# Attention with an octonion FFN on one Trainium2 core: score stacks filled in strided rows, and the q and k weights loaded behind the store of the parts

## The chip, the cores and the metric

The kernel runs as one program on one core of a Trainium2 chip. The metric is the device time of one execution in microseconds (us). "PE" is TensorE's matmul, "PEld" its weight load, "DVE" VectorE, "ACT" ScalarE, "POOL" GpSimd and "SP" SyncE, which in this kernel does little but issue DMA transfers.

## The reference, cut to what matters

Two sequences of 1024 tokens with 512 features go through a layer norm; the result feeds causal attention of 32 heads of 16 features with an ALiBi bias, and a feed-forward network whose weights are ternary and multiplied as octonions. The output is `x + s * g`.

```python
xn = _layernorm(x)                                    # x: 2 x 1024 x 512
# attention, 32 heads of 16
qkv = jnp.einsum('bsd,od->bso', xn, w_qkv) + b_qkv
scores = jnp.einsum('bqhd,bkhd->bhqk', q, k) * (1 / sqrt(16))
scores = scores + slopes[h] * positions[k]            # ALiBi
scores = jnp.where(causal, scores, -1e9)
out = softmax(scores) @ v
s = jnp.einsum('bsd,od->bso', out, w_out) + b_out
# feed-forward network
h = silu(oct_ternary_linear(xn, w_gate)) * oct_ternary_linear(xn, w_up)
g = silu(oct_ternary_linear(h, w_down))
x = x + s * g
```

## The kernel before

**Work and units.** The attention is cut into units (b, g, qc): sequence b, group g of four heads (eight groups), half qc of the 1024 queries. There are 32 units. For each unit PE computes scores twice. The first pass (line 553, tiles `s1`, in the profile `s<-k_stack,q_stack`) serves only the row maxima, which DVE takes (`mx`, `left`). The maxima are turned by PE (line 618, `pm`), copied by ACT (`mr`) and written by a DMA that POOL issues into rows 126 and 127 of the query stack. The second pass (line 669, tiles `s2`, with a mask product at line 688 for blocks on the diagonal) then has scores less their maximum, and ACT takes the exponentials `p`. Line 707 multiplies `p` by `v`, and line 776 is the output projection. After the attention come the products of the network (lines 1436 and 1478).

**Stacks.** A score is a product over a stack of rows. `q_stack` (a ring of 4) and `k_stack` (a ring of 5) hold 128 partitions x 4 heads x 512 tokens. Rows 0 to 63 are four parts of 16 rows each: high and low parts of q or k, so that high x high, high x low, low x high and low x low are added up in one product. Rows 64 and 65 hold the ALiBi bias in two parts, and rows 126 and 127 the maxima. The order of the 64 rows is free as long as both stacks have the same.

**Where the rows come from.** `qk_items` (line 461) computes q and k of a set, which is two groups of one sequence. There are eight sets, n = 0 to 7. A set has four blocks (q and k, each in two halves of 512 tokens), and a block has four matmuls (line 477, tile `pqk`). After a block ACT adds the bias and rounds to the high part, DVE computes the low part (both go to `st`), and SP stores the block to DRAM (`sp<-st`, 512 KB). `fill_k` (line 514) and `fill_q` (line 527) read from there: four transfers of 128 KB on SP for one stack half, each 16 partitions x 4 heads x 512 tokens in pieces of 2 KB, and for `k_stack` one more for the bias rows.

**Weights of a set.** `load_wq` (line 143) issues two transfers of 512 KB on SP into `wqr`. `compact_wq` (line 151) has POOL copy them in eight pieces into `wq`, which the matmuls read; it is called ahead of the first product of the set. Both tiles have a single buffer. The load for set n + 1 is issued in `product`, at the last product of set n.

**What sets the order.** Every engine runs its instructions in the order of the program. That order is decided while the program is built by a planner written out in Python: at each step it looks at the candidates (a maximum's product, an exponential's product, a value product, a transpose, a side item such as a product of `qk_items`) with an estimate of when each is ready, and emits one. Its clock is `now`, in ns. For a fill it keeps `link`, the estimate of when the fill has gone out on the DMA link, and `fill_at`, when the stack can be read; `next_max` places a product of the first pass no earlier than `fill_at` of its stack. The planner has no estimate for the weights in `wqr`. Fills are issued by `try_fill` (line 1136).

Of the kernel before, what the change touches and what calls it, by code (L numbers as in the profile page):

```python
# [10 lines left out]
F32 = mybir.dt.float32  # L11
# [8 lines left out]
B, S, D = 2, 1024, 512  # L20
NT = B * S
H, HD = 32, 16
NG = H // 4
KD = D // P
# [51 lines left out]
def kernel(  # L76
# [21 lines left out]
    act_, dve_, pool_, sp_ = (  # L98
        InOrder(tc, engine, held) for engine in (nc.scalar, nc.vector, nc.gpsimd, nc.sync)
    )  # L100
# [3 lines left out]
    def pe(ins):  # L104

        return tc.keep_in_program_order(ins)

    NP = NG // 2
# [34 lines left out]
    def load_wq(gp, eng):  # L143
        t = wqp.tile([P, 2, KD, 2, 4, 32], F32, tag="wqr", name=f"wqr_{gp[0]}_{gp[1]}")
        for n in range(2):
            eng.dma_start(
                out=t[:, n].rearrange("p k w h e -> p (k w h e)"), in_=wqk[2 * gp[1] + n]
            )
        wq_raw[gp] = t

    def compact_wq(gp):
        t = wq_raw.pop(gp)
        w = wqp.tile([P, KD, 2, P], F32, tag="wq", name=f"wq_{gp[0]}_{gp[1]}")
        for n in range(2):
            for k in range(KD):
                pool_.tensor_copy(
                    w[:, k, :, n * 64 : (n + 1) * 64].rearrange("p w (h d) -> p w h d", d=HD),
                    t[:, n, k, :, :, 0:HD],
                )
        wq_tiles[gp] = w  # L160
# [59 lines left out]
    for n in range(2):  # L220
        pool_.dma_start(
            out=bqk_sb[n * 64 : n * 64 + 64, 1 - n : 1 - n + 2 * NG],
# [183 lines left out]

    def q_of(b, g, half):
        return q_ring[(2 * (b * NG + g) + half) % 4]  # L410

    def k_of(b, g, half):
        return k_ring[(2 * (b * NG + g) + half) % 5]
# [47 lines left out]
    def qk_items(b, gp):  # L461

        box = {}

        def product(which, c, kt):
            if (which, c, kt) == (0, 0, 0):
                if (b, gp) not in wq_tiles:
                    compact_wq((b, gp))
                parts[b, gp] = [
                    spill.tile([2, P, S], F32, tag=f"sp{w}", name=f"sp_{b}_{gp}_{w}")  # L470
                    for w in range(2)
                ]
            if kt == 0:
                box["ps"] = ps_m.tile([P, 512], F32, tag="m", name=f"pqk_{b}_{gp}_{which}_{c}")
            ps = box["ps"]
            pe(
                nc.tensor.matmul(  # L477
                    ps,
                    lhsT=wq_tiles[b, gp][:, kt, which, :],
                    rhs=xnT[:, kt, b * S + c * 512 : b * S + (c + 1) * 512],  # L480
                    start=(kt == 0),
                    stop=(kt == KD - 1),
                )
            )
            n = b * NP + gp + 1
            if (which, c, kt) == (1, 1, KD - 1) and n < B * NP:
                load_wq((n // NP, n % NP), sp_)
            if kt < KD - 1:
                return
            bias = bqk_sb[:, 1 + 2 * (which * NP + gp) :][:, 0:1]  # L490
            st = stg.tile([P, 2, 512], F32R, tag="st", name=f"st_{b}_{gp}_{which}_{c}")
            act_.activation(st[:, 0, :], ps, AF.Identity, bias=bias)
            dve_.scalar_tensor_tensor(
                st[:, 1, :], ps, bias, st[:, 0, :].bitcast(F32), ALU.add, ALU.subtract
            )
            sp_.dma_start(
                out=parts[b, gp][which][:, :, c * 512 : (c + 1) * 512].rearrange(
                    "l p n -> p l n"
                ),
                in_=st.bitcast(F32),  # L500
            )

        return [
            (858, lambda w=w, c=c, kt=kt: product(w, c, kt), "qk" if kt == KD - 1 else None)
            for w in range(2)
            for c in range(2)
            for kt in range(KD)
        ]

    def heads(t, l, g, first, n):  # L510
        lo = (g % 2) * 64
        return t[l, lo : lo + 64, first : first + n].rearrange("(h d) n -> d h n", d=HD)

    def fill_k(b, g, half):

        k = k_of(b, g, half)
        for r in range(4):
            sp_.dma_start(
                out=k[r * HD : (r + 1) * HD].bitcast(F32),
                in_=heads(parts[b, g // 2][1], r % 2, g, half * 512, 512),  # L520
            )
        sp_.dma_start(
            out=k[64:66].bitcast(F32),
            in_=al_dram[:, 4 * g : 4 * g + 4, half * 512 : half * 512 + 512],
        )

    def fill_q(b, g, half):

        q = q_of(b, g, half)
        for r in range(4):  # L530
            sp_.dma_start(
                out=q[r * HD : (r + 1) * HD].bitcast(F32),
                in_=heads(parts[b, g // 2][0], r // 2, g, half * 512, 512),
            )

# [2 lines left out]
    def max_items(b, g, qc):  # L538
# [7 lines left out]
        def products(tl, first, count, c, n):  # L546
            x_banks[0] += 1
            ps = ps_x.tile(
                [P, 512], F32, tag=f"x{x_banks[0] % 3}", name=f"s1_{b}_{g}_{4 * qc + tl}_{c}_{first}"
            )  # L550
            for j in range(count):
                pe(
                    nc.tensor.matmul(  # L553
                        ps[:, j * n : (j + 1) * n],
                        lhsT=q_of(b, g, qc)[0 : NR - 2, first + j, tl * P : (tl + 1) * P],
                        rhs=k_of(b, g, c)[0 : NR - 2, first + j, :n],
                        start=True,
                        stop=True,
                    )
                )  # L560
            return ps[:, 0 : count * n].rearrange("p (h n) -> p h n", n=n)
# [50 lines left out]
    def place_max(b, g, qc, tiles):  # L612

        q = q_of(b, g, qc)
        ps = ps_m.tile([P, 512], F32, tag="m", name=f"pm_{b}_{g}_{qc}")
        for tl in range(4):
            pe(
                nc.tensor.transpose(  # L618
                    ps[0:8, tl * P : (tl + 1) * P],
                    tiles["rm"][:, tl].rearrange("p l h -> p (l h)"),  # L620
                    ident,
                )
            )
        mr = wk.tile([8, 512], F32R, tag="mr", name=f"mr_{b}_{g}_{qc}", bufs=1)
        act_.copy(mr, ps[0:8, :])
        for n in range(2):
            pool_.dma_start(
                out=q[NR - 2 + n : NR - 1 + n].bitcast(F32),
                in_=mr[4 * n : 4 * n + 4, :].bitcast(F32),
            )  # L630
# [218 lines left out]
    def unit_of(lst, n):  # L849
        return lst[n][0] if n < len(lst) else NU  # L850

    for b in range(B):
        for hh in range(2):
            n = 2 * b + hh
# [11 lines left out]
        for gp in range(2 - 2 * b, NP):  # L866
            n = b * NP + gp
            u = 4 * n
            add(
                qk_items(b, gp),  # L870
                u - 6 if n > 1 else -1,
                u - 3,
                lambda b=b, n=n: n < 2 or fills[0] >= 4 * (2 * n - 2) and (b == 0 or not waits_x()),
            )
# [23 lines left out]
    for n in order:  # L898
        if n in seen:
            continue  # L900
        k = n
# [90 lines left out]

    busy(20)
    qk, vs = qk_items(0, 0), v_items(0, 0)

    def issue(items):
# [62 lines left out]
    lead_in += [(d // 4, None, it) for d, it in zip(due, vs)]  # L1059
    head_v = len(lead_in)  # L1060
    lead_in += [(size[0] + 4 * d, None, it) for d, it in zip(due[::2], qk_items(0, 1))]
    known["l", "g"] = 36000
    known["k", "u"] = 42000
# [43 lines left out]
    now, kind = [HEAD], ["F"]  # L1107
# [3 lines left out]
    p_ready, placed, fill_at = {}, {}, []  # L1111
    link = [0.0]
# [20 lines left out]
    qk_done = [HEAD + 4500]  # L1133

    def try_fill():

        n, part = divmod(fills[0], 4)
        if n >= B * NG or len(qk_done) <= (n // 2 + 1 if n > 1 else part // 2):
            return
        if n == 0 and now[0] < qk_done[part // 2] - 4000:  # L1140
            return
        if unit_of(exps, E[0]) < 2 * (n - 2) + (0, 1, 2, 2)[part]:
            return
        (fill_q if part % 2 else fill_k)(n // NG, n % NG, part // 2)
        fills[0] += 1
        link[0] = max(now[0], link[0], qk_done[n // 2 + 1 if n > 1 else part // 2]) + (4500 if n else 3000)
        fill_at.append(link[0] + 2500)

    def try_fetch():
        for n, k in enumerate(fetches):  # L1150
# [213 lines left out]
    while E[0] < len(exps) or V[0] < len(vals) or S_[0] < len(side) or norms or behind:  # L1364
        try_fill()
        try_fetch()
        if not w_again and unit_of(exps, E[0]) >= NU - 5:
            fetch_signs()
        if not step():
            now[0] += 500  # L1370
            assert now[0] < 1e8
# [245 lines left out]
```

## Time and profile before

| | |
|---|---|
| median of 3 runs | 1092.06 us (1090.71 to 1093.07) |
| profiled execution | 1090.84 us, its span 1089.0 us |
| mean granted TensorE clock | 0.98 of full speed |
| DVE, ACT, POOL busy | 678.9, 508.3, 173.8 us |
| DMA | 104.04 MB, mean 96 GB/s over the span |
| fills | 128 transfers of 128 KB each into `k_stack` and into `q_stack` |
| weights | 16 transfers of 512 KB into `wqr` |

The span runs from the first to the last instruction; the rest of the profiled execution's time lies around it. Times inside the profile count from the start of the span. A wait is idle time of an engine just before an instruction, put down to what released that instruction. The granted clock is the share of full speed that TensorE got in a stretch. The DMA share is the mean busy share of the core's 16 DMA engines, GB/s what they moved.

The attention's first units run from about 37 us on; the products of the network's output end the span. All 32 stores of `st` lie between 19 and 650 us.

### The profile page before, as it was taken

Reading aid. Unit: us, or ns where it says so; the run is one execution under the profiler, and the core shown is the slowest. Engines: PE = TensorE matmul, PEld = TensorE weight load, DVE = VectorE, ACT = ScalarE, POOL = GpSimd, SP = SyncE. Lnnn points to the kernel's source line nnn. Section 1 sums busy time; section 2 is a strip of 40 time slices with the busy share of each in tenths; the row PEclk is TensorE's granted clock in tenths of the full one; section 3 lists DMA queues with packets and bytes.
Section 4 is the critical chain, followed back from the end, with each engine's and each line's share of the span. In section 5 each row is a group of like instructions: output and inputs, shape, how many; then the busy total and the mean of one; then the engine's idle time right before and its main releaser. Section 6 shows DMA issues by size and latency. Waiting matters only on the chain.

```text
span 1089.0 us, 15459 instructions
## 1 busy us (share of the span) xinstructions
PE 1036.4 (95%) x5578; PEld 696.3 (64%) x5578; DVE 678.9 (62%) x1406; ACT 508.3 (47%) x958; POOL 173.8 (16%) x288
## 2 busy tenths in 40 slices
PE   8798988998999999999999999999999999999995
PEld 5554656674666667556667566665456678888784
DVE  6668888774988867878878778858342123141312
ACT  4032647654665544555645455665581213232322
POOL 7501014001010011010011000010011123332322
PEclk9999979999999999999999999999999999999998
DMA  6986563525374454355354337741141113030211
GB/s 226 175 157 161 137 124 108 89 52 116 82 154 89 123 85 81 99 136 95 74 128 65 82 78 116 137 89 50 35 132 49 49 59 116 1 116 1 79 38 39
DMA packets 73195, 104.04 MB, mean 96 GB/s; under 512 B 25896, under 2 KB 30640, under 8 KB 73120
## 3 DMA queue, kind: packets, MB, share of 16 engines
q1 hardware_dynamic: 69648, 98.28, 40.2%
q0 software_dynamic: 3424, 4.64, 1.7%
q8 instruction: 45, 0.74, 0.3%
q14 instruction: 30, 0.25, 0.1%
q10 hardware_dynamic: 48, 0.13, 0.0%
HBM read 69.39 MB, written 33.10 MB: 94 GB/s over the span
## 4 chain that ended last, share of the span: by engine, by line
PE 76%; DVE 8%; issue 5%; DMA 5%; ACT 4%; POOL 2%; SPq 0%; DVEq 0%; POOLq 0%; ACTq 0%
PE po L707 12%; PE s L669 12%; PE s L553 11%; PE pqk L477 9%; PE pu L1436 6%; PE pg L1436 6%; PE pd L1478 6%; PE pout L776 5%; PE pv L435 4%; DVE mx L69 3%; PE s L688 2%; DMA q_stack<-mr 1%; ACT p L69 1%; PE pm L618 1%; DVE s L69 1%
## 5 line engine op out<-in xcount | busy, mean ns | idle before, releaser
L69 ACT ACTIVATE p<-s 128x512 f32<-128x512 f32 x576 | 317.5, 596 | 205.0 <-PE s L688 114.0
L669 PE MATMUL s<-q_stack,k_stack 128*128 128x512 f32 (+3 forms) x768 | 252.5, 397 | 10.3 <-ACT p L69 5.1
L553 PE MATMUL s<-k_stack,q_stack 126*128 126x512 f32 (+3 forms) x768 | 235.5, 391 | 15.3 <-DVE mx L69 7.7
L69 DVE TENSOR_REDUCE mx<-s 128x1 f32<-128x384 f32 (+3 forms) x352 | 226.2, 643 | 11.6
L69 DVE TENSOR_REDUCE left<-s 128x1 f32<-128x512 f32 x256 | 163.8, 684 | 49.7 <-PE s L553 49.3
L669 PEld LDWEIGHTS s<-q_stack,k_stack 128*128 128x128 f32 x768 | 133.1, 190 | 82.7 <-ACT p L69 37.3
L553 PEld LDWEIGHTS s<-k_stack,q_stack 126*128 126x128 f32 x768 | 131.3, 192 | 67.5 <-issue 23.0
L707 PE MATMUL po<-p,v 128*32 128x512 f32 (+3 forms) x1536 | 142.2, 492 | 0.4 <-ACT p L69 0.4
L69 DVE TENSOR_TENSOR s<-s,mask 128x128 f32<-128x128 f32 (+2 forms) x352 | 123.9, 352 | 29.0 <-PE s L553 28.1
L477 PE MATMUL pqk<-xnT,wq 128*128 128x512 f32 x256 | 132.3, 618 | 8.1 <-POOL wq L69 6.9
L69 DVE SCALAR_TENSOR_TENSOR h<-pu,sc_u,sg 128x512 f32<-128x512 f32 (+1 forms) x44 | 33.0, 751 | 156.6 <-PE pu L1436 155.6
L69 POOL DMA_DIRECT2D q_stack<-mr x64 | 32.2, 508 | 615.5 <-ACT mr L69 615.5
L69 POOL TENSOR_TENSOR hs<-h,hs 128x512 fp32r<-128x512 f32 (+1 forms) x43 | 56.3, 1310 | 215.5 <-ACT hs L69 215.5
L688 PE MATMUL s<-mask_r,ident_r 128*128 128x256 f32 (+1 forms) x320 | 89.0, 278 | 0.0
L707 PEld LDWEIGHTS po<-p,v 128*32 128x32 f32 x1536 | 42.3, 109 | 72.5 <-issue 65.3
L69 ACT ACTIVATE sg<-pg,sc_g 128x512 f32<-128x512 f32 (+1 forms) x44 | 30.2, 687 | 100.2 <-PE pg L1436 100.0
L435 PE MATMUL pv<-wv,xnT 128*128 128x256 f32 x256 | 68.3, 392 | 0.1
L477 PEld LDWEIGHTS pqk<-xnT,wq 128*128 128x128 f32 x256 | 46.4, 195 | 33.8 <-issue 20.3
L69 ACT CAST hs<-h 128x512 fp32r<-128x512 f32 (+1 forms) x44 | 27.2, 619 | 85.3 <-DVE h L69 85.3
L776 PE MATMUL pout<-wo_sb,oT 128*128 128x512 f32 x128 | 62.7, 604 | 0.5 <-ACT oT L69 0.5
L688 PEld LDWEIGHTS s<-mask_r,ident_r 128*128 128x128 f32 x320 | 60.5, 189 | 2.7 <-issue 1.7
L435 PEld LDWEIGHTS pv<-wv,xnT 128*128 128x128 f32 x256 | 47.0, 193 | 17.1 <-issue 8.4
(144 smaller groups left out, 1074.8 us busy)
## 6 DMA issues: line engine op xcount, KB each, us to landing
sp<-st SPq DMA_DIRECT2D x32, 512.0 KB
k_stack<-sp SPq DMA_DIRECT2D x128, 128.0 KB
q_stack<-sp SPq DMA_DIRECT2D x128, 128.0 KB
wqr<-in_wqk_dram SPq DMA_DIRECT2D x16, 512.0 KB
xt<-in_x_dram SPq DMA_DIRECT2D x16, 256.0 KB
att<-o SPq DMA_DIRECT2D x32, 128.0 KB
ot<-att SPq DMA_DIRECT2D x16, 256.0 KB
proj<-y SPq DMA_DIRECT2D x16, 256.0 KB
```

Of the source, the lines that this page charges most:

```text
L69: ins = issue(*args, **kwargs)
L435: nc.tensor.matmul(ps[:, 0:256], lhsT=xnT[:, c, b * S + kt * P : b * S + (kt + 1) * P], rhs=wv_tiles[2 * b + hh][:, c, :], start=(c == 0), ...
L477: nc.tensor.matmul(ps, lhsT=wq_tiles[b, gp][:, kt, which, :], rhs=xnT[:, kt, b * S + c * 512 : b * S + (c + 1) * 512], start=(kt == 0), st ...
L553: nc.tensor.matmul(ps[:, j * n : (j + 1) * n], lhsT=q_of(b, g, qc)[0 : NR - 2, first + j, tl * P : (tl + 1) * P], rhs=k_of(b, g, c)[0 : NR ...
L618: nc.tensor.transpose(ps[0:8, tl * P : (tl + 1) * P], tiles["rm"][:, tl].rearrange("p l h -> p (l h)"), ident,)
L669: nc.tensor.matmul(ps[:, c0 : c0 + w], lhsT=k_of(b, g, kt // 4)[0:NR, h, kt % 4 * P : (kt % 4 + 1) * P], rhs=q[0:NR, h, 512 - w : 512], st ...
L688: pe(nc.tensor.matmul(out, lhsT=ident_r, rhs=rhs, start=False, stop=True))
L707: nc.tensor.matmul(po[32 * i : 32 * i + 32, 512 - w : 512], lhsT=v[:, kt, h * VC : h * VC + 32], rhs=p[:, i * part + c0 : i * part + c0 + ...
L776: nc.tensor.matmul(ps, lhsT=turned[t][:, c, :], rhs=wo_sb[0][:, c, :], start=(c == 0), stop=(c == KD - 1),)
L1436: nc.tensor.matmul(ps[:fs, :], lhsT=fw[mt][:, n0 + kt, 0:fs], rhs=part[:, kt, :], start=(kt == 0 and n == 0), stop=(kt == KD - 1 and n == 1),)
L1478: nc.tensor.matmul(pd, lhsT=hs[k][:fs, n, st * P : (st + 1) * P], rhs=fw[mt][:fs, 8:12, :].rearrange("p s n -> p (s n)"), start=(mt == 0 a ...
```

## The change

Three things change. The four transfers of a fill no longer write 16 consecutive rows each: transfer r writes rows r, r + 4, r + 8 and so on up to r + 60, in both stacks alike. The load of the next set's weights is issued after the store of the last block instead of before its bias, low part and store. And the planner's estimates for a fill get shorter: `link` moves by 2600 ns a fill instead of 4500 (3000 for the first group), and the stack counts as readable 2200 ns after that instead of 2500.

```diff
@@ qk_items, product
-            n = b * NP + gp + 1
-            if (which, c, kt) == (1, 1, KD - 1) and n < B * NP:
-                load_wq((n // NP, n % NP), sp_)
             if kt < KD - 1:
                 return
             bias = bqk_sb[:, 1 + 2 * (which * NP + gp) :][:, 0:1]
...
                 in_=st.bitcast(F32),
             )
+            n = b * NP + gp + 1
+            if (which, c, kt) == (1, 1, KD - 1) and n < B * NP:
+                load_wq((n // NP, n % NP), sp_)
@@ fill_k
         for r in range(4):
             sp_.dma_start(
-                out=k[r * HD : (r + 1) * HD].bitcast(F32),
+                out=k[r:64:4].bitcast(F32),
                 in_=heads(parts[b, g // 2][1], r % 2, g, half * 512, 512),
             )
@@ fill_q
         for r in range(4):
             sp_.dma_start(
-                out=q[r * HD : (r + 1) * HD].bitcast(F32),
+                out=q[r:64:4].bitcast(F32),
                 in_=heads(parts[b, g // 2][0], r // 2, g, half * 512, 512),
             )
@@ try_fill
         fills[0] += 1
-        link[0] = max(now[0], link[0], qk_done[n // 2 + 1 if n > 1 else part // 2]) + (4500 if n else 3000)
-        fill_at.append(link[0] + 2500)
+        link[0] = max(now[0], link[0], qk_done[n // 2 + 1 if n > 1 else part // 2]) + 2600
+        fill_at.append(link[0] + 2200)
```

Since the planner works with these estimates, the order of the other instructions on every engine moves as well; their number on PE stays the same.

## The prediction

> **What bounds the kernel now.** I read the page's busy times first, then PE's waits over two stretches, then the windows around the fills and around the waits, then the chain and SyncE's timeline.
>
> Busy times (engine, us, share of the span, instructions):
>
> ```profile
> PE 1036.4 (95%) x5578; PEld 696.3 (64%) x5578; DVE 678.9 (62%) x1406; ACT 508.3 (47%) x958; POOL 173.8 (16%) x288
> ```
>
> PE is the bound; only 1089.0 - 1036.4 = 52.6 us of its span are idle, so an edit on another engine pays only where PE stands still or runs at half clock. PE's waits from 0 to 260 us (who, on what: us in total, times, longest), then from 260 to 715:
>
> ```profile
> PE pqk L477 <- POOL wq L69: 5.8, 2, 3.2
> PE s L553 <- DMA q_stack<-sp: 5.6, 2, 5.2
> PE s L669 <- DMA q_stack<-mr: 4.2, 2, 2.4
> ```
>
> ```profile
> PE pqk L477 <- POOL wq L69: 1.1, 1, 1.1
> ```
>
> A fill (`q_stack<-sp`) makes PE wait only near the start, and between 260 and 715 us it never does: there the fills are hidden, and whatever new wait the change puts there is lost whole. The windows of the fill stage (window, its length, busy time and count of PE, PEld, DVE, ACT, POOL; then granted clock, DMA share, GB/s):
>
> ```profile
> 31.00:36.00 5.00, 5.00 (x24) 4.24 (x23) 1.60 (x3) 0.69 (x1) 4.95 (x3) 1.00 1.06 135
> 36.50:40.50 4.00, 4.00 (x24) 3.48 (x23) 2.67 (x5) 0.00 (x0) 3.51 (x39) 1.00 1.04 416
> 45.00:53.00 8.00, 2.84 (x11) 1.69 (x11) 6.61 (x14) 0.00 (x0) 0.00 (x0) 0.95 1.07 131
> ```
>
> All DMA engines are busy in all three, but while fills run (31 to 36, 45 to 53) only 131 to 135 GB/s move, and 416 while other loads run. A fill of 512 KB takes 512 KiB / 131 GB/s = 4.0 us. Behind PE's waits the clock falls:
>
> ```profile
> 53.05:59.00 5.95, 5.95 (x13) 3.80 (x13) 3.18 (x8) 0.00 (x0) 0.00 (x0) 0.50 1.06 130
> 93.20:96.60 3.40, 3.40 (x5) 1.51 (x5) 1.48 (x3) 0.00 (x0) 0.66 (x3) 0.50 0.95 251
> 249.44:254.00 4.56, 4.56 (x8) 2.02 (x9) 0.00 (x0) 0.00 (x0) 0.66 (x3) 0.63 0.44 61
> 477.43:482.00 4.57, 4.57 (x26) 2.79 (x26) 2.85 (x5) 2.66 (x5) 0.66 (x3) 1.00 1.02 253
> ```
>
> These follow PE waits of 5.20, 2.62, 3.18 and 1.08 us: the first leaves 6 us at half clock (3.0 us lost), the next two 3.4 us each (1.7 lost), the last nothing. The chain (start, length) shows what the early waits stand on, and SyncE's timeline how stores and weight loads are queued:
>
> ```profile
> 33.79 8.37 DMA sp<-st
> ...
> 62.50 7.97 DMA q_stack<-mr
> ...
> 87.18 5.62 DMA wqr<-in_wqk_dram
> ```
>
> ```profile
> 86.26 0.36 SPq L69 DMA_DIRECT2D sp<-st  x1
> 86.71 1.29 SPq L69 DMA_DIRECT2D wqr<-in_wqk_dram  x2
> 92.61 0.38 SPq L69 DMA_DIRECT2D sp<-st  x1
> ```
>
> The store of set 0's last block, issued at 33.79, landed at 42.16 because two slow fills and 1 MB of `wqr` were ahead of it, and the next fills start only then. At 62.5 a `mr` transfer of 8 KB took 7.97 us behind six fills (median landing 2.3 in the list of issues). And `wqr` is on the path already: issued at 86.71, landed at 92.80, first of it copied into `wq` by POOL, PE running again at 93.20. The next store went out only at 92.61, after it; the change turns these two round.
>
> **Part 1, strided rows.** Same instructions and bytes; only the partitions of each of the four transfers differ. No row shows this pattern. One end: nothing changes (131 GB/s). Other end: as fast as the other loads, 416 GB/s. I take a doubling, 262 GB/s and 2.0 us a fill: the 16 consecutive rows now lie four times as far apart, and issuing a fill takes SyncE 1.75 us (42.18 to 43.91 for four), so beyond a doubling the issue itself would bound.
>
> [...]
>
> What it gives at the start: together with part 2 the store of 33.79 no longer stands behind 1 MB of weights (2.5 us at 416 GB/s) and two fills are 4 us shorter; it lands near 37, and unit 1's first fills by about 45 instead of 52.8. PE's wait of 5.20 and the half clock after it go, and so does most of the 7.97 us of `mr`. What is late next is DVE: its timeline runs without a gap from 38.1 to 51.8 us on unit 0's maxima, and only then are `rm`, PE's transpose (0.6), ACT's `mr` (0.6), POOL's issue (0.9) and a landing of 2.3 to 4 us possible. That puts the first product of the exponentials (L669) at 57 to 60, I take 58.6, instead of 70.6: 12.0 us earlier, less 1.3 us of PE work that the new order leaves for later: **-10.7**. Bounds: -8.0 (landing and order 2.7 worse) to -13.3 (57.3, and nothing left over).
>
> **Part 2, the load behind the store.** In the built order each of the seven later `wqr` loads stands behind the last store of its set on SyncE, and that store waits for ACT and DVE. Rows for the path from the last product of a set to PE's next restart: ACT 0.69, DVE 0.75, issue 0.1 (together 1.54; 2.68 to 2.87 in the first two sets); store to next issue 0.46 (92.61 to 93.08); load, issue to landing 6.1 (86.71 to 92.80; other sets 5.3 to 6.2 by their last packet); copies until PE runs 0.4. So 8.5 us, early 9.8. All of it is hidden where the order puts that much PE work between two sets; queued behind the held products on PE are the scores of the next units, so ACT and DVE starve too. At four of the seven boundaries there is enough (the wait of 3.18 us ahead of set 3 is not one on the load: POOL stands there behind a `mr` transfer in both orders, and it stays). At three there isn't:
> - Set 1 to 2: one score product in between (0.2 us). Wait 8.3 to 9.6, I take 8.8, instead of 2.62: **+6.2**. Half clock follows in both; 0 to 1.7 more.
> - Set 3 to 4: the new order leaves 12 value products (1.7 us by the row of 2.29 for 16), 4 transposes (0.5), 5 products of L669 and 2 masks (1.3), 3 of L553 (0.7), 4.2 us in all; wait 8.5 - 4.2, I take 4.1 (3.5 to 5.6) and 1.7 of half clock: **+5.8**. Before, no wait.
> - Set 5 to 6: 4 products of L669, 2 masks and 3 short ones of L553, 1.5 us; wait 7.0 instead of 1.08, and 1.7 of half clock (3.4 if it falls as behind 5.20): **+7.6** (6.8 to 9.3).
>
> [...]
>
> **Part 3, the planner's constants.** They cost no instruction; they let a score product be placed 4.8 us (2600 + 2200 ns) behind a fill's issue, where it was 7.0 (4500 + 2500). With fills 2.0 us shorter this is safe in the sum. PE has the same 4461 instructions in the built order, three fewer changes into value products; -0.6 at most. From 137 to 205 us, where PE stands in small waits that end on DVE or `mr` (one of 1.78), the faster `mr` and fills give **-1.5** (0 to -3). The rest, with another tail of the attention after 720 us: **-1.0** (-2.8 to +2; new fill waits up to +3).
>
> **Sum.** -10.7 + 6.2 + 5.8 + 7.6 - 1.5 - 1.0 = +6.4 us. On the profiled execution (1090.84 us: span 1089.0 and 1.84 around it) that is 1097.2. The median of the runs, 1092.06, lies 1.2 above the profiled one, so on its basis **1098.4 us**. All terms at their best: -13.3 + 5.7 + 5.2 + 6.8 - 3.0 - 2.8 = -1.4, or 1090.7; at their worst -8.0 + 8.7 + 7.3 + 9.3 + 5 = +22, which needs all to go wrong at once.
>
> **Rivals.**
> 1. *Faster: the start gives much more.* Elapsed time less PE's work stands at 24.7 us at 88 us, 6.7 of it from before the first score product. If all the other 18.0 went, and 5.0 of the small waits from 137 to 205 us, the sum is -18.0 - 5.0 - 1.0 + 19.6 = -4.4, or 1087.7. It decides from a start gain of 17 us on. For it: DMA is saturated from 43 to 66 us. Against: DVE's unbroken row to 51.8 us.
> 2. *The same: gain and stalls cancel*, within 2.2 us of 1092.06 (0.2%, about what a measurement of this kernel can tell from no change). With every load at 5.3 us the three stalls cost 17.7 by the ends above, and with the best start it is -13.3 + 17.7 - 1.5 - 1.0 = +1.9, or 1094.0; for it: the load of set 6 in the trace of before took 5.3. Against: both ends at once.
> 3. *The fills don't get faster.* Then the start gives only the 2.5 us of weights ahead of the store, and the constants are too early by up to 2.2 us a unit where a fill is late: -2.5 + 19.6 + 0 to 5, or 1109 to 1114. For it: all DMA engines are busy already during fills, with nothing in the trace that says why they are slow. Against: other loads reach 416 with the same engines.
> 4. *The load behind the store isn't felt*, because the next products are placed far enough away: the order shows it for four boundaries, not for three; included in rivals 1 and 2.
>
> **How the numbers follow.** My sum 0.64, rival 1 0.20, rival 2 0.10, rival 3 0.06. The forecast's own range is 1094.5 to 1104, from the ends of the start gain and of the three stalls, not all at once. The range for 8 in 10 takes in rival 2 and most of rival 1: 1087.5 to 1105.5. Slower is the forecast and rival 3: 0.70; same 0.10; faster 0.20.
>
> **What would show it.** Right: some 260 GB/s in the windows of fills; no `s <- DMA q_stack<-sp` near 50 us; first L669 near 58.6; `pqk <- POOL wq` grown from 6.9 us in three waits to some 23 us in four, each new one at a set boundary and followed by half clock. Wrong: a start gain over 17 us, 131 GB/s as before, or waits on `wq` under 10 us in total.

## The result and the profile after

The changed kernel takes 1099.42 us (median of 4 runs, 1098.8 to 1099.56) against 1091.99 us for the kernel before (4 runs, 1090.71 to 1093.07): 1.0067 times as long, 95% interval 1.005 to 1.0085. The forecast was 1098.4 us and slower. The profiled execution took 1099.45 us, its span 1097.7.

Busy times of the changed kernel (engine, us, share of the span, instructions):

```profile
PE 1035.5 (94%) x5578; PEld 695.7 (63%) x5578; DVE 678.7 (62%) x1406; ACT 508.6 (46%) x958; POOL 173.5 (16%) x288
```

PE runs the same 5578 instructions in a span that is 8.7 us longer. Its busy time is 0.9 us less and its idle time grows from 52.6 to 62.2 us, so the loss is time in which PE stands still. Its waits from 0 to 260 us and, in the second fence, from 260 to 715 (who, on what: us, times, longest). The line numbers are higher by one:

```profile
PE pqk L478 <- POOL wq L69: 13.2, 2, 9.9
PE s L554 <- DVE mx L69: 4.6, 5, 2.5
PE s L554 <- DVE rm L69: 1.9, 1, 1.9
```

```profile
PE pqk L478 <- POOL wq L69: 14.3, 3, 7.6
```

The waits on `q_stack<-sp` and `q_stack<-mr` are no longer in the list; those on `wq` have grown from 6.9 us in three to 27.4 (13.2 + 14.3 with rounding) in five. They stand at the set boundaries that were named, as PE's timeline shows (start, length, instruction, in brackets the idle time before it and who ended it; from set 1 to 2, 3 to 4, 5 to 6):

```profile
91.05 1.22 PE L478 MATMUL pqk<-xnT,wq 128*128 128x512 f32 x1 [9.90 <-POOL wq L69]
...
304.52 2.08 PE L478 MATMUL pqk<-xnT,wq 128*128 128x512 f32 x2 [5.17 <-POOL wq L69]
...
485.81 2.08 PE L478 MATMUL pqk<-xnT,wq 128*128 128x512 f32 x2 [7.57 <-POOL wq L69]
```

The windows (PE, PEld, DVE, ACT, POOL busy; clock, DMA share, GB/s) show two stretches of fills and then the half clock around these three waits, part of which lies in the waits themselves (PE is busy for 4.47, 6.04 and 5.65 us of them):

```profile
45.70:51.00 5.30, 3.41 (x16) 2.66 (x15) 5.16 (x11) 0.00 (x0) 0.00 (x0) 1.00 0.56 176
51.00:57.00 6.00, 6.00 (x26) 3.74 (x25) 5.86 (x12) 0.58 (x1) 1.09 (x2) 1.00 0.54 171
85.28:95.52 10.24, 4.47 (x7) 2.41 (x8) 0.87 (x3) 0.00 (x0) 2.00 (x8) 0.50 0.86 219
303.73:310.56 6.83, 6.04 (x19) 3.35 (x20) 1.28 (x2) 1.73 (x4) 2.31 (x6) 0.50 1.04 253
481.23:491.46 10.23, 5.65 (x16) 2.77 (x17) 0.91 (x3) 1.67 (x3) 2.00 (x8) 0.50 0.77 201
```

Fills now move 171 to 176 GB/s at a DMA share of 0.55, where they moved 131 at 1.07: the DMA engines are no longer the bound. In the trace's packets from 45 to 57 us the median 2 KB packet takes 84 ns instead of 264. What bounds a chain of fills now is their issue, in SyncE's timeline:

```profile
33.77 1.04 SPq L69 DMA_DIRECT2D sp<-st  x2
34.91 2.05 SPq L69 DMA_DIRECT2D wqr<-in_wqk_dram  x2
39.09 2.51 SPq L69 DMA_DIRECT2D k_stack<-sp  x4
...
45.70 2.52 SPq L69 DMA_DIRECT2D k_stack<-sp  x4
```

Four transfers of a fill take 2.5 us to issue; in the kernel before it was 1.73 (at 42.18 us). The median issue of `k_stack<-sp` went from 424 to 593 ns. The store's landing releases the fill at 39.09; before, it was 42.18.

Half clock in the whole span did not grow. Here are, for the kernel before and then for the changed one, the longest stretch between 140 and 180 us and the sum of all stretches at half clock ahead of the kernel's end (six and five windows):

```profile
147.82:161.47 13.65, 12.44 (x41) 8.27 (x43) 11.76 (x23) 8.47 (x19) 1.88 (x4) 0.50 0.31 100
...
sum 34.12, PE 31.94 PEld 19.11 DVE 21.25 ACT 12.47 POOL 3.12; mean PE 5.32 PEld 3.18 DVE 3.54 ACT 2.08 POOL 0.52
```

```profile
146.72:153.55 6.83, 5.50 (x18) 4.03 (x19) 6.37 (x16) 5.82 (x14) 1.62 (x2) 0.50 0.85 271
...
sum 37.56, PE 25.10 PEld 14.85 DVE 9.45 ACT 9.81 POOL 7.94; mean PE 5.02 PEld 2.97 DVE 1.89 ACT 1.96 POOL 1.59
```

PE does 25.1 us of its work at half clock, where it did 31.9. What lies around the three waits, 16.2 us, is outweighed by what is gone elsewhere. By this alone PE's busy time would be 3.4 us less, and it is 0.9 less; the other 2.5 us no run explains.

### The profile page after: what moved, and what is told of

It is laid out like the page before. It is cut to its first block, busy times and chain, and to the rows that moved or that the text cites. A ratio compares the mean times of both kernels' runs of the same rounds, so it can differ in the third digit from the quotient of the medians.

```text
span 1097.7 us, 15493 instructions
## 1 busy us (share of the span) xinstructions
PE 1035.5 (94%) x5578; PEld 695.7 (63%) x5578; DVE 678.7 (62%) x1406; ACT 508.6 (46%) x958; POOL 173.5 (16%) x288
## 5 line engine op out<-in xcount | busy, mean ns | idle before, releaser
L554 PE MATMUL s<-k_stack,q_stack 126*128 126x512 f32 (+3 forms) x768 | 239.2, 391 | 10.7 <-DVE mx L69 7.2
L478 PE MATMUL pqk<-xnT,wq 128*128 128x512 f32 x256 | 133.3, 620 | 28.6 <-POOL wq L69 27.4
```

Source lines behind the costliest of these rows:

```text
L478: nc.tensor.matmul(ps, lhsT=wq_tiles[b, gp][:, kt, which, :], rhs=xnT[:, kt, b * S + c * 512 : b * S + (c + 1) * 512], start=(kt == 0), st ...
L554: nc.tensor.matmul(ps[:, j * n : (j + 1) * n], lhsT=q_of(b, g, qc)[0 : NR - 2, first + j, tl * P : (tl + 1) * P], rhs=k_of(b, g, c)[0 : NR ...
```

## Where the time went, run by run

For each milestone the table gives how far a kernel stands behind the kernel before (negative: ahead). It is the start of that instruction in the trace less the PE work that stands ahead of it in that kernel's order, and the difference of the two kernels. The work of an instruction is the mean, for its tiles and shape in the trace of before, of the time from its start to its end or to the next start, whichever comes first. The experiments of the columns are told in the next section.

| milestone (time in the kernel before) | changed | rows alone | late load alone | rows + estimates | estimates alone | load late once |
|---|---|---|---|---|---|---|
| first L669 (70.6) | -9.6 | -4.6 | -2.8 | -4.3 | +0.9 | -9.6 |
| first L669 of the second unit (105) | -2.9 | -6.1 | +5.3 | -4.6 | +1.8 | -8.7 |
| first L669 of the sixth unit (205) | -6.0 | -5.2 | +5.2 | -5.9 | -0.7 | -10.3 |
| first L669 of the tenth unit (305) | -5.7 | -5.2 | +5.1 | -5.5 | -0.2 | -9.8 |
| first product of set 5 (423) | +4.5 | -5.3 | +5.1 | -1.5 | +3.7 | -5.8 |
| first product of set 7 (595) | +13.9 | -5.3 | +14.4 | -2.0 | +3.3 | -6.3 |
| first product of the network (802) | +8.6 | -6.1 | +15.9 | -7.4 | -2.2 | -11.7 |
| span | +8.7 | -6.1 | +15.9 | -7.3 | -2.1 | -11.7 |

PE runs the same instructions in every kernel, so in the last two rows the figure is the plain difference of the times. In the rows above them, where the new estimates are in, it depends by up to 1 us on how overlapping instructions are charged.

## The experiments

**1. Rows alone.** The kernel before with `k[r:64:4]` and `q[r:64:4]`; every engine's order is that of before.

```diff
-                out=k[r * HD : (r + 1) * HD].bitcast(F32),
+                out=k[r:64:4].bitcast(F32),
```

> The kernel before with the strided rows alone; old place of the weight load, old estimates of the planner, so the order on every engine is that of before. Theory (the rows bring the gain at the start, the late load brings the loss): the wait of 5.20 us near 48 us and the half clock behind it go, the first product of L669 comes near 60 instead of 70.6, nothing new waits behind the set boundaries (2.6 or less, 3.2, 1.1 us). About 1079 us, 1076 to 1084. Rival (the rows give little without the store going ahead of the weights): 1086 to 1090, with a wait on q_stack<-sp of 2 us or more left near 48 us.

1083.6 us against 1091.03, ratio 0.994 (0.9907 to 0.9972): faster, but short of 1079, and the first L669 comes at 65.97 instead of near 60. The wait on `q_stack<-sp` is gone, and another stands in its place:

```profile
PE s L553 <- DVE rm L69: 4.2, 1, 4.2
```

In the old order PE's next product waits for DVE's unbroken row to end, still with 6.8 us of half clock around its end (4.8 of them PE's work). And the store of the last block of set 0 landed no sooner, though the fills ahead of it were fast (SyncE's timeline of this run, then of the changed kernel and of experiment 2):

```profile
36.12 0.41 SPq L69 DMA_DIRECT2D sp<-st  x1
44.08 2.45 SPq L69 DMA_DIRECT2D k_stack<-sp  x4
```

```profile
34.41 0.40 SPq L69 DMA_DIRECT2D sp<-st  x1
```

```profile
33.52 0.38 SPq L69 DMA_DIRECT2D sp<-st  x1
...
40.85 1.78 SPq L69 DMA_DIRECT2D k_stack<-sp  x4
```

From the store's issue to the fill that its landing releases it is 8.0 us here, after 8.4 before. With slow fills and the weights behind the store (experiment 2) it is 7.3, and with both changes 4.7 (34.41 to 39.09). Either one alone, the slow fills or the 1 MB of weights, holds the store up.

**2. Late load alone.** The kernel before with `load_wq` moved behind the store; PE's order is that of before.

```diff
-            if (which, c, kt) == (1, 1, KD - 1) and n < B * NP:
-                load_wq((n // NP, n % NP), sp_)
...
                 in_=st.bitcast(F32),
             )
+            if (which, c, kt) == (1, 1, KD - 1) and n < B * NP:
+                load_wq((n // NP, n % NP), sp_)
```

> The kernel before with the load behind the store alone; slow fills, old estimates, same order of PE's instructions as before. Theory: wait from set 1 to 2 of 8.5 to 9.5 us (2.62 before), from set 3 to 4 none or under 1 us, since 10 us or more of work lie between, from set 5 to 6 some 7 us (1.08 before) and half clock behind; the first fills start 2 to 3 us earlier. About 1103 us, 1099 to 1107. Rival (the late load costs nothing by itself, the new order does): 1088 to 1093.

1105.86 us, ratio 1.0134 (1.0102 to 1.0165). Waits from 0 to 260 us, then from 260 to 720:

```profile
PE pqk L477 <- POOL wq L69: 14.2, 2, 11.0
```

```profile
PE pqk L477 <- POOL wq L69: 9.0, 1, 9.0
```

11.0 us from set 1 to 2 (3.2 of the 14.2 is the old wait ahead of set 3), 9.0 from 5 to 6, nothing from 3 to 4: in the places expected, each some 2 us longer than I had it. The first fills start at 40.85, 1.3 us earlier and not 2 to 3.

**3. No late load.** The changed kernel with the load at its old place; PE's order is that of the changed kernel.

> The changed kernel with the load back ahead of the last block's store; strided rows and new estimates stay, and PE's order is that of the changed kernel. Theory: the waits on wq of 9.90, 5.17 and 7.57 us shrink to 2 to 4, 0 to 2 and 0 to 2 us, and their half clock goes; the gain at the start stays. About 1080 us, 1076 to 1085. Rival (the order of the new estimates is what costs, the load only shows it): 1090 us or more.

1082.08 us, ratio 0.9915 (0.9883 to 0.9947). Waits from 0 to 260 us, then from 260 to 720:

```profile
PE pqk L478 <- POOL wq L69: 6.6, 2, 3.3
...
PE s L554 <- DMA q_stack<-sp: 4.5, 1, 4.5
```

```profile
PE pqk L478 <- POOL wq L69: 3.0, 2, 1.5
```

The order of the changed kernel is the same in both, so the late load costs some 17 us in it (1.0067 - 0.9915 = 1.5% of 1092). That the gain at the start stays was wrong, and this shows what the late load gives: without it the wait on the fills near 47 us is back and the lead at the first L669 is 4.3 instead of 9.6.

**4. Estimates alone.**

```diff
-  + (4500 if n else 3000)
-        fill_at.append(link[0] + 2500)
+  + 2600
+        fill_at.append(link[0] + 2200)
```

> The kernel before with the planner's new estimates alone: the order of the changed kernel with slow fills and the load at its old place. Theory: fills at 131 GB/s are later than the planner takes them to be, so PE waits for q_stack<-sp or k_stack<-sp near the start (5 to 8 us) and in some units later; no gain at the start. About 1095 us, 1091 to 1102. Rival (the estimates make the gain, since they put products in a better order): 1085 us or less.

1087.03 us, ratio 0.9961 (0.9935 to 0.9987): the rival's sign, and my expectation of 1095 was wrong. The waits that I expected near the start are there, but they only take the place of the old ones:

```profile
PE s L553 <- DMA q_stack<-sp: 4.8, 1, 4.8
...
PE s L669 <- DMA q_stack<-mr: 3.3, 1, 3.3
```

No fill is waited for later. The gain comes in the tail of the attention: the table's column falls from +3.3 at set 7 to -2.2 at the network. PE does not stand still for less time than before (53.4 us against 52.6), but it does 20.9 us of its work at half clock, where it was 31.9; which part of that belongs to the order and which to the run that was profiled stays open.

**5. Old estimates.** The changed kernel with 4500 (3000) and 2500 again.

> The changed kernel with the planner's old estimates: strided rows and the late load, PE's order that of the kernel before. If rows and late load together make the gain at the start and the estimates have no part in it, the first product of L669 comes near 60 us; the set boundaries then wait as in the run with the late load alone (about 11 us from set 1 to 2, none from 3 to 4, 9 from 5 to 6): about 1097 us, 1094 to 1101. If the new order is needed for the gain at the start, the first L669 stays at 64 to 66 and the time is 1100 or more.

1098.97 us, ratio 1.008 (1.0053 to 1.0107). The first L669 comes at 62.35 us, between the two cases; its lead of 8.3 us is most of the 9.6, and the new order adds the rest. The waits on `wq` are 9.5 us from set 1 to 2 and 7.9 from 5 to 6, 1.5 and 1.1 us shorter than with slow fills (experiment 2, same order).

**6. Late load once.** The changed kernel, but only the load for set 1 stays behind the store; the others go back ahead of it.

```diff
+            n = b * NP + gp + 1
+            if (which, c, kt) == (1, 1, KD - 1) and 1 < n < B * NP:
+                load_wq((n // NP, n % NP), sp_)
             if kt < KD - 1:
                 return
...
-            if (which, c, kt) == (1, 1, KD - 1) and n < B * NP:
+            if (which, c, kt) == (1, 1, KD - 1) and n == 1:
```

> The changed kernel with the late load for the first set's successor only (set 1's weights behind the store of set 0); the six later loads ahead of the store as before. If the late load gives some 5 us at the start by letting the store of 33.8 go ahead of 1 MB of weights, and takes them back at the later boundaries: first L669 at 59 to 60 us, waits on wq of 2 to 4 us from set 1 to 2, 1.5 or less from 3 to 4 and from 5 to 6; about 1077 us, 1073 to 1080, faster than both kernels and than either part left out. If the start gain is given back by 105 us to DVE anyway: 1081 to 1084, as with no late load at all.

1077.18 us, ratio 0.9872 (0.9844 to 0.99): the lead of 9.6 at the first L669 is still 9.8 at 305 us (table), and the waits on `wq` are 6.7 and 3.0 us in all as without any late load.

**7. Six loads a block earlier.** As 6, with `(1, 0, KD - 1)` in place of `(1, 1, KD - 1)` for the six.

> As the run before it, but the six later loads a block earlier still (at the last product of the first k block). The weights then have some 5 us more: the waits on the load from set 1 to 2 (2 to 4) and from 3 to 4 (1.5) go, those where POOL stands behind a transfer of mr (3.3 near 238 us, 1.5 near 418) stay. About 1074 us, 1070 to 1078. If an earlier load delays the stores and fills queued behind it instead, waits on fills or on mr appear and the time is 1079 or more.

1073.81 us, ratio 0.9848 (0.982 to 0.9875). The wait from set 1 to 2 fell from 3.40 to 1.89 us; the one from 3 to 4 (1.51) did not move, so the load was not its cause. POOL's timeline there:

```profile
288.61 1.00 POOL L69 DMA_DIRECT2D q_stack<-mr  x2 [13.59 <-ACT mr L69]
289.60 1.93 POOL L69 COPY wq<-wqr 128x128 f32<-128x128 f32 x8
```

The copies stand behind two `mr` transfers that wait for ACT.

**8. The copies ahead.** As 7, with `compact_wq` of those six sets behind the last store of the set before, in program order.

> As the run with the six later loads a block earlier, and POOL's eight copies of those six sets into wq are issued at the end of the set before (behind its last store in the program) instead of ahead of the next set's first product. In the run before it the waits of 1.89, 3.26, 1.51 and 1.53 us all have POOL busy with two transfers of mr just ahead of the copies. If these stand in the way, the four waits and the half clock behind two of them go: about 1065 us, 1062 to 1069. If the copies then hold up mr transfers behind them on POOL instead, waits of L669 on q_stack<-mr appear and the time is 1071 or more.

1065.15 us, ratio 0.9752 (0.9728 to 0.9776), the fastest of all. From 260 to 720 us PE waits for no copy any more; before that one wait is left:

```profile
PE pqk L478 <- POOL wq L69: 1.9, 1, 1.9
```

Three of the four waits went, and this one from set 1 to 2 did not. There the `mr` product stands ahead of set 1's last product even now, so that POOL issues `mr` from 82.65 to 83.64 us and copies after that; set 1's last product ends at 82.85, and `wq` has a single buffer, so even without `mr` the copies could start only 0.8 us earlier.

**9. Another pattern of rows.** Experiment 3 with every second of 32 rows, to see whether the distance between the rows sets how fast a fill is.

```diff
-                out=k[r:64:4].bitcast(F32),
+                out=k[r // 2 * 32 + r % 2 : r // 2 * 32 + 32 : 2].bitcast(F32),
```

> The changed kernel without the late load, with another pattern of rows: transfer r writes every second of 32 rows (16 rows in rows 0 to 31 or 32 to 63) instead of every fourth of 64. [...]

1081.01 us, ratio 0.9908 (0.9886 to 0.993), against 0.9915 with every fourth row. The median 2 KB packet from 45 to 57 us takes 84 ns in both. Between a distance of two rows and one of four the runs show no difference.

## Why the prediction was right, point by point

| step | forecast | measured (trace, or steps worked out as in the table) |
|---|---|---|
| first L669 at | 58.6 us | 59.24 us |
| gain at the start | -10.7 | -9.6 |
| set 1 to 2: wait; cost | 8.8; +6.2 | 9.90; +6.7 (-9.6 to -2.9) |
| 137 to 205 us | -1.5 | -3.1 (-2.9 at 105 us to -6.0 at 205) |
| set 3 to 4: wait; cost | 4.1; +5.8 | 5.17; +8.5 (-5.7 to +2.8 at the eleventh unit) |
| set 4 to 5 | 0 | 1.53; +2.2 |
| set 5 to 6: wait; cost | 7.0; +7.6 | 7.57; +9.0, and 0.3 more by 595 us |
| the rest | -1.0 | -5.3 in the tail (+13.9 at 595 us to +8.6 at the network) |
| sum | +6.4 | +8.7 (span) |

**The start** came out in size, but not with the shares that its working gave. Rows alone lead by 4.6 us at the first L669, the late load alone by 2.8, both together by 8.3 (experiment 5) and by 9.6 in the new order. The working blamed two slow fills and 1 MB of weights for the store's 8.37 us and added their shares up. With fast fills alone the store still took 8.0, with the weights behind it alone 7.3, with both 4.7: the blame was right, but the shares do not add up, and the term "2.5 us at 416 GB/s" for the weights is 1.1 with slow fills ahead and 3.3 with fast ones. Rows and load need each other.

**The fill** was put at 262 GB/s and runs at 171 to 176. The step that failed took the issue for a fixed 1.75 us; it is 2.5 with strided rows. The sum did not suffer, because its next bound was DVE, which holds: the one wait left near 47 us is on `rm`, 1.9 us. The median 2 KB packet takes 84 ns in both strided patterns (experiment 9) and 264 with consecutive rows; what makes the difference no run shows. From 176 GB/s at a DMA share of 0.56 I estimate 314 GB/s with all DMA engines busy (176 / 0.56); no run shows fills without the bound of their issue.

**The stalls** were right in place and 0.6 to 1.1 us short each in length. The term that was short is the load: 6.1 us from issue to landing, where the second half of the weights now lets POOL go on 6.9 us after the issue from set 1 to 2 (83.82 to 90.70, POOL's timeline):

```profile
88.91 1.00 POOL L69 COPY wq<-wqr 128x128 f32<-128x128 f32 x4 [7.14 <-DMA wqr<-in_wqk_dram]
90.70 1.00 POOL L69 COPY wq<-wqr 128x128 f32<-128x128 f32 x4 [0.79 <-DMA wqr<-in_wqk_dram]
```

The transfer runs together with the fills queued behind it, and slow fills there make the waits longer still (11.0 and 9.0 us in experiment 2, 9.5 and 7.9 in experiment 5). The half clock was as large a miss: PE works 4.47, 6.04 and 5.65 us at half clock around the three waits, where about 3.4 was taken for each, and half of the excess, some 3 us in all, is lost. Where 19.6 us were forecast for the three, 24.2 were measured. One wait wasn't seen at all, the 1.53 us from set 4 to 5: in both kernels the copies stand behind `mr` there, but only the new order has PE arrive early enough to wait.

**The estimates** were taken for harmless or costly; alone they gain 4 us (experiment 4). Two terms hang on the order that they make. "Rest, -1.0" was mis-sized: the tail gives -5.3, and it does so with the new order in other kernels too (-5.4 and -5.5 in experiments 3 and 4), but not in the old one (-0.8 and +1.5 in experiments 1 and 2). And the -1.5 from 137 to 205 us was put down to faster `mr` and fills, which is not where it came from: with them in the old order the lead shrinks there (experiment 1, -6.1 to -5.2), with slow fills in the new order it grows (experiment 4, +1.8 to -0.7). What changes most there is the half clock, 15.7 us of PE's work between 147 and 176 us before and 5.5 after. These two terms came out 5.9 us better than forecast, the stalls, the unseen wait and the start 7.9 worse. That the total came within 1.0 us of the forecast is luck; that the loss at three boundaries outweighs the gain at the start is not.

**The rivals.** "The start gives much more" fell: -9.6, not -18. "Gain and stalls cancel" fell too, since the stalls cost 24.2 us and not 17.7. "The fills don't get faster" fell with the packets (84 ns instead of 264). "The load isn't felt" held at four boundaries and fell at three, as the order said.

## What to carry to other kernels

When a transfer is moved behind another on the same queue, list for every place what now stands between its issue and its first use: the same move gave 5.3 us at the first boundary, where the queue was the bound, and cost some 17 us net. Move it only where it pays (1077.18 us with one of seven moved), and then look at what the consumer really waits for: the last two steps to 1065.15 us were an earlier load and copies put ahead of another engine's traffic. A single buffer whose refill is issued at its last use has no slack except the work that happens to lie between.

## What the runs showed of the hardware

- In the traces every stretch at half clock, but for the one at the kernel's end, lasted a multiple of 3.41 us: 3.41, 6.83, 10.24 or 13.65. A wait of 2.62 us, the one from set 1 to 2 in the kernel before, was followed by one of 3.41 us.
- In each trace all these stretches began on one grid of 3.41 us (kernel before: 52.25, 93.21, 147.82, 171.72, 250.22 and 762.22 us). From 20 us on, and up to 12 us before the end, all 36 windows of that grid at full clock in which PE was busy for less than 43% were followed by half clock, in all eleven kernels together; of those between 43 and 90%, 19 were and 190 were not (kernel before: 5 of 5 and 1 of 20; changed kernel: 5 of 5 and 0 of 21). Two waits of much the same length lie differently to the grid: from set 1 to 2 the 2.62 us of the kernel before lie in one window, with half clock behind it, and the 2.55 us of experiment 1 are split over two, with none (the first row is the kernel before):

```profile
89.80:93.21 3.41, 0.66 (x5) 0.31 (x3) 3.24 (x9) 0.67 (x1) 1.37 (x6) 1.00 0.63 232
```

```profile
84.11:87.53 3.42, 2.02 (x10) 1.16 (x9) 3.25 (x9) 0.69 (x1) 0.19 (x1) 1.00 0.95 301
87.53:90.94 3.41, 2.13 (x6) 1.18 (x7) 2.79 (x6) 0.00 (x0) 1.81 (x8) 1.00 0.60 198
90.94:94.35 3.41, 3.41 (x14) 1.79 (x13) 2.00 (x5) 1.26 (x2) 1.00 (x2) 1.00 0.65 200
```

- The same wait of 1.44 to 1.47 us near 100 us (`pm` on DVE) was followed by 3.41 us at half clock in experiments 3 and 6 and by none in the changed kernel or in experiments 4, 7, 8 and 9. In these two PE was busy for 57 and 58% of the window that has the wait, in the five others for 59% or more; but elsewhere a window of 55% was not followed by half clock (changed kernel, 423.2 us), so what decides it no run shows. Waits of the same length thus cost different amounts in these runs, and that may be part of the spread of the kernel before (1085.02 to 1096.56 us over 14 runs beside experiments 1 to 4).
- Issuing a transfer of 16 strided partitions took 593 ns on SyncE, of 16 consecutive ones 424 (median of the 128 `k_stack<-sp` in the changed kernel and in the kernel before), with the same bytes and pieces. The stride is not all of it: the transfer of the bias rows behind them, whose rows did not change, went from 288 to 443 ns.
